# Weight-factor stores moved to GpSimd's queue, and a denser schedule of side work in the first attention

## The chip, the cores and the metric

One core of a Trainium2 chip runs the whole program. Its engines work side by side: TensorE (PE) multiplies matrices, VectorE (DVE) and ScalarE (ACT) do elementwise work, GpSimd (POOL) does a little of it and can issue DMAs, and SyncE (SP) does nothing but issue DMAs. The metric is the device time of one execution in microseconds (us). Before the change the median of three runs is 3205.84 us (3205.17 to 3208.25).

## The reference

The input x has 8 images of 512 channels and 32x32 positions (1024 tokens). Two layers of the same form follow each other; only the weights differ:

```python
xn  = group_norm(x, 8 groups) * gamma + beta
q, k, v = Wq @ xn + bq, Wk @ xn + bk, Wv @ xn + bv       # 512 x 512 each, 1024 tokens
attn = softmax(q_h^T k_h * 64**-0.5)                      # 8 heads of 64 channels
x   = x + Wp @ (attn @ v) + bp
```

All is float32. Eight images and two layers make 16 such jobs, and the kernel does them one after the other, two images at a time: layer 0 of images 0 and 1, then layer 1 of both, and so on.

## The kernel before

**Products by Strassen's scheme.** The four weight products of a job are done with seven block products in place of eight (Winograd's form), and for Q, K and the output projection O this is done twice, one level inside the other. That needs sums and differences of weight blocks ("factors") and of data blocks ("sums"). Four DVE subtractions or additions make the factors of a weight (`factor`, lines 154 to 160, parts 0 to 3). The first time a weight is used they are made from the raw blocks and stored to device memory (`store_factors`, L165 and L168); later `fetch` (L190) loads them into a ring of seven weight tiles. The factors of the second level are made in the ring the first time (`prepare`) and are stored by L204.

**Attention** (`class Attention`). A job's attention has 64 steps: 8 groups (head pair by half of the tokens) of 8 key blocks. Step i has four 64x512 score products (`sc`, L870), one exponential on ACT (`e`, L875), one addition on DVE that sums the exponentials over the key blocks (`acc`, L885 for the first of a group, L887 after it), and four products with the values two steps later (`po`, L901). The `e` tiles come from a pool of six, so that the exponential of step i+6 has to wait until the addition and the value products of step i have read theirs. At the end of a group `finish` reduces `acc` (L917) and adds the two halves of `po` (L924). After every second group the sums of 128 partitions are put together by three small DMAs (`r<-r`, L944), inverted on DVE (L948, L949), written to device memory (`rd`, L961), read back broadcast (`rb`, L963, two DMAs) and multiplied in (L978).

**Side work of an attention** (`chores`). The main loop gives each attention a table from step number to a piece of side work; `put(i, fn)` places a piece at step i, or at the next free step after it. For the first attention (n = 0) the table holds, in the order of placing: loading two raw weights (O of layer 0, V of layer 1) at step 2; their eight factor parts and two stores (`first_factors`); the statistics of the next job's group norm, which in this job alone are made on ACT (`reads`: four sums, the means, four sums of squares, and then one piece with a DVE scaling L258 and `gather`); and then `steps + sums`: `groups`, `factors` of the norm (L304 to L306), four ACT instructions that apply the norm (L311), and four DVE differences of blocks of the normalised input (`combine`, L385 to L391). Four inner differences (`inner_sums`, L423 to L429) come last.

**The chain of the group norm.** `gather` writes the statistics to device memory with two DMAs (`dm`, L275) and reads them back by groups (`gm`, L279). `groups` starts with a DVE instruction on `gm` (L286), ends with a power on GpSimd (L291), and its result goes out and back again (`dg`, L293; `mr`, L296) to the norm's factors (L304).

**Order.** The instructions of PE, ACT and DVE stand in the order in which the Python code issues them. Those of SP and POOL are ordered by the framework, from its own estimate of when each can run; every engine then works through its list strictly in order, and an instruction whose input is not there holds up all behind it on that engine.

Of the kernel before, what the change touches and what calls it, by code (L numbers as in the profile page):

```python
# [40 lines left out]
K, V, Q, O = range(4)  # L41
# [31 lines left out]
def fast_path(  # L73
# [10 lines left out]
    nc = tc.nc  # L84
# [23 lines left out]
    def later(delay, fn):  # L108
        todo.append((clock[0] + delay, fn))
# [36 lines left out]
    def load_blocks(w, layer, which):  # L146
        for i in range(2):
            for j in range(2):
                nc.sync.dma_start(w[:, 2 * j + i], raw_block(layer, which, i, j))

    def factor(w, part):

        if part == 0:
            nc.vector.tensor_add(w[:, S1], w[:, S3], w[:, A22])
        elif part == 1:
            nc.vector.tensor_sub(w[:, S2], w[:, S1], w[:, A11])  # L156
        elif part == 2:
            nc.vector.tensor_sub(w[:, S3], w[:, A11], w[:, S3])
        else:
            nc.vector.tensor_sub(w[:, S4], w[:, A12], w[:, S2])  # L160

    def store_factors(w, layer, which):
        keep = wdram.tile([P, NW, 2, CH], F32, name=f"keep_{which}_{layer}")
        if (which, layer) == (O, 1):
            nc.sync.dma_start(keep, w)  # L165
        else:
            for s in (slice(S1, NW), slice(S3, S3 + 1)):
                nc.sync.dma_start(keep[:, s], w[:, s])  # L168
        factors[which, layer] = keep

    plan, held, raw = deque(), {}, set()
# [1 line left out]
    def fetch():  # L173


        if not plan or len(held) == RING:
            return
        key = plan.popleft()
        n, which, o = key
        layer = jobs[n][1]  # L180
        w = ring.tile([P, NW, P], F32, tag="w", name=f"w_{which}_{n}_{o}")
        held[key] = w
        if (which, layer, o) in deep:
            nc.sync.dma_start(w, deep[which, layer, o])
        else:
            if o in BLOCK:
                src = raw_block(layer, which, *BLOCK[o])
            else:
                src = factors[which, layer][:, FACTOR[o]]
            nc.sync.dma_start(wide(w), src)  # L190
            if which != V:
                raw.add(key)
# [20 lines left out]
    def x_tile(b):  # L213
        xs[b] = xpool.tile([P, NC, S], F32, tag="x", name=f"x_{b}")
        return xs[b]

    def load_x(b):
        for cc in range(NC):
            nc.sync.dma_start(xs[b][:, cc, :], x[b, cc * P : (cc + 1) * P, :])

    class Norm:
# [20 lines left out]
        def sums(self, cc):  # L242

            nc.scalar.activation(
                xn[0][:, cc, :], xs[self.b][:, cc, :], AF.Identity, accum_out=self.mv[:, cc, 0:1]
            )
# [523 lines left out]
    def last_weights(n):  # L770
        w = acts.tile([P, NW, 2, CH], F32, tag="deep", name="w_last")
        nc.sync.dma_start(w, factors[O, jobs[n][1]])
        return w
# [10 lines left out]
    def last_sums(sh):  # L784


        def start():
            if sh == 0:
                tx[0] = acts.tile([P, 3, 2, HALF], F32, tag="t", name="t_last")
            nc.vector.tensor_sub(last_right(sh, 5), last_right(sh, 7), last_right(sh, 1))  # L790

        def second():
            nc.vector.tensor_sub(last_right(sh, 6), last_right(sh, 3), last_right(sh, 5))

        def third():
            nc.vector.tensor_sub(last_right(sh, 7), last_right(sh, 3), last_right(sh, 7))

        def fourth():
            nc.vector.tensor_sub(last_right(sh, 4), last_right(sh, 2), last_right(sh, 6))

        return start, second, third, fourth
# [241 lines left out]
    def deep_steps(n):  # L1043


        made = []

        def sums_(part, direct):
            if not made:
                made.append(True)  # L1050
                d = acts.tile([P, 4, 7, QT], F32, tag="deep", name=f"deep_{n}")
                deep_x[0], deep_t[0] = d[:, :, :4, :], d[:, :, 4:, :]
            inner_sums(part, direct)

        return [
            lambda part=part, direct=direct: sums_(part, direct)
            for direct in (True, False) for part in range(4)
        ]

    def extend_plan(n):  # L1060
        plan.extend((n, V, o) for o in ORDER)
        plan.extend((n - 1, O, o) for o in ORDER)
        plan.extend((n, which, o) for which in (K, Q) for o in OUTER)
# [29 lines left out]

        return load, [lambda oc=oc: add_up(oc) for oc in range(NC)]

    def first_factors(put, which_layers):

        box = []

        def start():  # L1100
            box.append(acts.tile([P, 2, NW, 2, CH], F32, tag="deep", name=f"raw_{len(factors)}"))
            for i, (which, layer) in enumerate(which_layers):
                load_blocks(box[0][:, i], layer, which)

        put(2, start)
        at = 9
        for i, (which, layer) in enumerate(which_layers):
            for part in range(4):
                at += 3
                put(at, lambda i=i, part=part: factor(box[0][:, i], part))  # L1110
            put(at + 1, lambda i=i, which=which, layer=layer: store_factors(
                box[0][:, i], layer, which
            ))

    deep_x, deep_t = [None], [None]
# [160 lines left out]
    for n in range(-1, len(jobs)):  # L1276
        last = n + 1 == len(jobs)
        outs = None
        if n >= 0:
            chores = {}  # L1280

            def put(i, fn):
                while i in chores:
                    i += 1
                chores[i] = fn

            if last:
                w = last_weights(n)
                for i, fn in enumerate(last_sums(0)):
                    put(44 + 3 * i, fn)  # L1290
            else:
                if n == 0:
                    first_factors(put, [(O, 0), (V, 1)])
                elif n == 1:
                    first_factors(put, [(K, 1), (Q, 1)])
                elif n == 2:
                    first_factors(put, [(O, 1)])
                for i, (_, fn) in enumerate(extra):
                    put(2 + i, fn)
                at = (10, 19, 22, 24, 26, 28, 36, 39, 42, 45)  # L1300
                if n == 0:
                    for i, fn in zip((3, 3, 4, 5, 6, 8, 10, 11, 12, 13, 15), reads):
                        put(i, fn)
                    at = (22, 30, 34, 35, 37, 38, 41, 44, 47, 50)
                for i, fn in zip(at, steps + sums(n + 1)):
                    put(i, fn)
                deep_first = deep_steps(n + 1)
                for at, fn in zip((52, 54, 57, 59), deep_first[4:]):
                    put(at, fn)
                put(61, lambda: (extend_plan(n + 1), [fetch() for _ in range(RING)]))  # L1310
            assert max(chores, default=0) < NT * len(att.groups)
            att.run(chores)
            banks(0, "one")
            banks(1, "one")
            if last:
                for i, fn in enumerate(last_sums(1)):
                    later(7.0 + 0.8 * i, fn)
                later(13.0, judge)
                for sh in range(2):
                    last_proj(n, w, sh)  # L1320
                break
            outs = OutputSums(n)
            out_sums(n, outs)
            first = v_phase(n + 1, ORDER)
            for thunk in first[:-1]:
                thunk()
            rest = first[-1:]
            extra = deque()
            if jobs[n][1] == 1 and jobs[n][0] + 2 < B:
                extra.append((11, lambda b=jobs[n][0] + 2: (x_tile(b), load_x(b))))  # L1330
            if n == 1:
                load, bias_steps = make_out_bias(1)
                extra.append((8, load))
                extra.extend((11, fn) for fn in bias_steps)
            if n + 2 < len(jobs):
                reads, steps = norm_steps(n + 2)
                extra.extend((15, fn) for fn in reads)
        both = deep_phases(n + 1, extra, outs, deep_first[:4] if outs else ())
        both[0]()
        rest[0]()  # L1340
        if n < 0:
            later(22.0, lambda: load_x(1))
        for thunk in both[1:]:
            thunk()
        banks(0, "two")
        att = Attention(n + 1)
        att.scores(0)
        att.scores(1)
        banks(1, "two")
        att.scores(2, "po")  # L1350
# [249 lines left out]
```

## Time and profile before

| what | value |
|---|---|
| median of three runs | 3205.84 us (3205.17 to 3208.25) |
| the profiled execution | 3206.06 us, span 3204.3 us |
| busy, of the span | PE 99%, DVE 87%, ACT 60%, POOL 3% |
| granted TensorE clock | 1.00 throughout |
| one attention, first score product to last value product | 109.6 us the first, 109.5 us all others |
| from there to the next attention's first score product | 96.0, 93.1, 90.6 us after the first three, 88.3 us after nearly all others |

The span is the time from the first to the last instruction of the program; the time of the execution holds 1.8 us more. Busy time is what instructions of an engine took together; an engine's "wait" is time in which it stood idle, put down to whatever ended it.

### The profile page before, as it was taken

The page shows a single profiled execution, that of the slowest core. Times are in us where ns is not written, and L with a number is a line of the kernel's source. Part 1 is how long each engine was busy: PE and PEld are TensorE (multiplying, and loading weights), DVE is VectorE, ACT ScalarE, POOL GpSimd, SP SyncE. Part 2 cuts the span into 40 slices and gives each one's busy share as a digit, 9 for nine tenths or more (in the row PEclk, how much of TensorE's full clock was granted, in tenths as well). Part 3 has the DMA queues.
Part 4 walks back from the last instruction along what each step waited for, and adds up shares of the span by engine and source line. Part 5 has one row for each costly group of instructions (what it writes and reads, how often), then busy time and mean ns, then how long its engine had stood idle before and what let it go on. Part 6 is the DMA issues. An engine that isn't in the chain of part 4 may idle for free.

```text
span 3204.3 us, 57789 instructions
## 1 busy us (share of the span) xinstructions
PE 3185.3 (99%) x22917; PEld 1862.8 (58%) x22917; DVE 2772.8 (87%) x3989; ACT 1914.4 (60%) x3063; POOL 100.7 (3%) x95
## 2 busy tenths in 40 slices
PE   9999999999999999999999999999999999999999
PEld 7366384563836638366483754837547375573744
DVE  8897999979889798897988879888898888978878
ACT  4746646466565665656656565565656656566564
POOL 0000000000000000000000000000000000000000
PEclk9999999999999999999999999999999999999999
DMA  8234172350613305034170421504316051150611
GB/s 291 74 107 127 48 213 70 92 169 22 210 28 88 91 26 159 22 100 132 33 211 16 114 72 33 152 16 135 103 44 194 16 137 48 49 136 16 174 37 42
DMA packets 156998, 308.32 MB, mean 96 GB/s; under 512 B 34104, under 2 KB 60592, under 8 KB 156464
## 3 DMA queue, kind: packets, MB, share of 16 engines
q1 hardware_dynamic: 139856, 272.05, 26.8%
q0 software_dynamic: 16864, 32.51, 6.2%
q8 instruction: 181, 2.97, 0.4%
q14 instruction: 97, 0.79, 0.1%
HBM read 225.13 MB, written 45.68 MB: 85 GB/s over the span
## 4 chain that ended last, share of the span: by engine, by line
PE 95%; DVE 3%; DMA 1%; issue 0%; POOL 0%; ACT 0%; DVEq 0%; ACTq 0%; POOLq 0%
PE sc L870 28%; PE po L901 27%; PE zd L636 10%; PE vd L636 10%; PE z L494 6%; PE yd L636 5%; PE ud L636 4%; PE v L494 2%; PE y L494 2%; PE u L494 1%; PE z_last L814 0%; DMA x<-p 0%; DVE w L156 0%; DMA w<-deep 0%; DVE p L655 0%; DVE v L520 0%
## 5 line engine op out<-in xcount | busy, mean ns | idle before, releaser
L875 ACT ACTIVATE e<-sc 128x1024 f32<-128x1024 f32 x1024 | 1045.3, 1025 | 563.4 <-PE sc L870 457.4
L870 PE MATMUL sc<-q,k 64*64 64x512 f32 x8192 | 1058.0, 589 | 0.0
L901 PE MATMUL po<-e,v 64*64 64x512 f32 x8192 | 1057.1, 589 | 0.0
L887 DVE TENSOR_TENSOR acc<-acc,e 128x1024 f32<-128x1024 f32 x768 | 936.0, 1219 | 58.8 <-ACT e L875 12.1
L901 PEld LDWEIGHTS po<-e,v 64*64 64x64 f32 x8192 | 312.9, 133 | 566.0 <-issue 554.4
L870 PEld LDWEIGHTS sc<-q,k 64*64 64x64 f32 x8192 | 311.2, 133 | 562.7 <-issue 545.0
L885 DVE TENSOR_TENSOR acc<-e,e 128x1024 f32<-128x1024 f32 x128 | 156.3, 1221 | 112.3 <-ACT e L875 112.2
L636 PE MATMUL zd<-deep,w 128*128 128x256 f32 x860 | 241.1, 380 | 3.8 <-DVE p L653 1.7
L636 PE MATMUL vd<-deep,w 128*128 128x256 f32 x804 | 224.3, 380 | 2.1 <-DVE p L655 1.3
L636 PEld LDWEIGHTS zd<-deep,w 128*128 128x128 f32 x860 | 162.8, 190 | 28.2 <-DVE p L653 3.0
L636 PEld LDWEIGHTS vd<-deep,w 128*128 128x128 f32 x804 | 152.3, 190 | 24.6 <-DVE p L655 2.5
L917 DVE TRANSPOSE_TENSOR_REDUCE r<-acc 128x32 f32<-128x1024 f32 x128 | 158.5, 1238 | 0.6
L682 POOL DMA_DIRECT2D x<-p x62 | 74.6, 1211 | 1972.7 <-ACT p L646 1525.2
L636 PE MATMUL vd<-os,w 128*128 128x256 f32 x420 | 118.1, 380 | 1.6 <-DVE p L655 1.5
L668 DVE TENSOR_TENSOR p<-p,p 128x1024 f32<-128x1024 f32 x94 | 114.2, 1214 | 0.0
L494 PE MATMUL z<-w,t 128*128 128x256 f32 x480 | 110.9, 379 | 0.0
L494 PE MATMUL z<-w,xn 128*128 128x256 f32 x480 | 110.1, 382 | 0.0
L518 ACT COPY v<-z 128x512 f32<-128x512 f32 x32 | 18.8, 586 | 148.7 <-PE z L494 148.7
L494 PEld LDWEIGHTS z<-w,xn 128*128 128x128 f32 x480 | 90.0, 190 | 23.8 <-issue 12.2
L442 ACT COPY ud<-zd 128x256 f32<-128x256 f32 x156 | 55.7, 357 | 76.6 <-PE zd L636 75.1
L653 DVE TENSOR_TENSOR p<-vd,s 128x256 f32<-128x256 f32 x63 | 26.7, 424 | 85.6 <-PE vd L636 85.6
L657 ACT COPY s<-vd 128x256 f32<-128x256 f32 x156 | 58.1, 373 | 69.2 <-PE vd L636 69.2
(242 smaller groups left out, 4194.9 us busy)
## 6 DMA issues: line engine op xcount, KB each, us to landing
w<-deep SPq DMA_DIRECT2D x287, 448.0 KB, 3.8
x<-p POOLq DMA_DIRECT2D x62, 512.0 KB, 6.9
rb<-rd SPq DMA_DIRECT2D x96, 256.0 KB, 4.0
w<-keep SPq DMA_DIRECT2D x84, 256.0 KB, 2.7
deep<-w SPq DMA_DIRECT2D x42, 448.0 KB, 3.8
w<-wqkv_dram SPq DMA_DIRECT2D x57, 256.0 KB, 2.8
x<-x_dram SPq DMA_DIRECT2D x28, 512.0 KB, 6.4
out_dram<-x SPq DMA_DIRECT2D x28, 512.0 KB, 6.2
```

Source lines behind the costliest of these rows:

```text
L442: nc.scalar.copy(u, z)
L494: nc.tensor.matmul(ps[:, ti * CH : (ti + 1) * CH], right(src, tx[0], o)[:, cc, t0 : t0 + P], w[:, cc, :], start=(start and ti == 0 and cc ...
L636: nc.tensor.matmul(ps, lhs[:, FACTOR[i], :], moving[i], start=start, stop=True, skip_group_check=True,)
L657: return chain(product, lambda ps: nc.scalar.copy(s5, ps), put, z, y, u, w)
L668: outer.append(lambda: nc.vector.tensor_add(to_, a, b))
L682: nc.gpsimd.dma_start(to_, p(part), accum_op=ALU.add)
L870: nc.tensor.matmul(sc[h * HD : (h + 1) * HD, j, :], k[r, hp, k0 : k0 + HD], q[r, hp, sh * HALF : (sh + 1) * HALF], start=True, stop=True,)
L875: nc.scalar.activation(e, sc, AF.Exp, scale=SCALE)
L885: nc.vector.tensor_add(acc[g], self.es[i - 1], e)
L887: nc.vector.tensor_add(acc[g], acc[g], e)
L901: nc.tensor.matmul(po[g][j * HD : (j + 1) * HD, h, :], v[r, kc, d0 : d0 + HD], e[r, j, :], start=(kc == 0), stop=(kc == NT - 1),)
L917: nc.vector.tensor_reduce(self.r[:, 0, m, :], self.acc.pop(g).rearrange("p j (b e) -> p (j b) e", e=RP), AX.X, ALU.add, apply_transpose=True,)
```

## The change

Three things change. `store_factors` takes the queue on which it issues, and the two or one stores per weight that the first three attentions make go to GpSimd's queue (five weights: two in the first, two in the second, one in the third); the three stores ahead of the first attention stay on SP. In the first attention the factor parts start at step 8 and come every second step (before: step 12, every third). And in the first attention the block differences and the inner differences of the next job are placed closer together and earlier.

```diff
-    def store_factors(w, layer, which):
+    def store_factors(w, layer, which, queue=nc.sync):
         keep = wdram.tile([P, NW, 2, CH], F32, name=f"keep_{which}_{layer}")
         if (which, layer) == (O, 1):
-            nc.sync.dma_start(keep, w)
+            queue.dma_start(keep, w)
         else:
             for s in (slice(S1, NW), slice(S3, S3 + 1)):
-                nc.sync.dma_start(keep[:, s], w[:, s])
+                queue.dma_start(keep[:, s], w[:, s])
         factors[which, layer] = keep
...
-    def first_factors(put, which_layers):
+    def first_factors(put, which_layers, at=9, apart=3):
...
         put(2, start)
-        at = 9
         for i, (which, layer) in enumerate(which_layers):
             for part in range(4):
-                at += 3
+                at += apart
                 put(at, lambda i=i, part=part: factor(box[0][:, i], part))
             put(at + 1, lambda i=i, which=which, layer=layer: store_factors(
-                box[0][:, i], layer, which
+                box[0][:, i], layer, which, nc.gpsimd
             ))
...
                 if n == 0:
-                    first_factors(put, [(O, 0), (V, 1)])
+                    first_factors(put, [(O, 0), (V, 1)], 6, 2)
...
                 if n == 0:
                     for i, fn in zip((3, 3, 4, 5, 6, 8, 10, 11, 12, 13, 15), reads):
                         put(i, fn)
-                    at = (22, 30, 34, 35, 37, 38, 41, 44, 47, 50)
+                    at = (22, 30, 34, 35, 36, 37, 39, 41, 43, 45)
                 for i, fn in zip(at, steps + sums(n + 1)):
                     put(i, fn)
                 deep_first = deep_steps(n + 1)
-                for at, fn in zip((52, 54, 57, 59), deep_first[4:]):
+                for at, fn in zip((47, 49, 51, 53) if n == 0 else (52, 54, 57, 59), deep_first[4:]):
                     put(at, fn)
```

## The prediction

> **What bounds the kernel now.** First the page's head:
>
> ```profile
> span 3204.3 us, 57789 instructions
> PE 3185.3 (99%) x22917; PEld 1862.8 (58%) x22917; DVE 2772.8 (87%) x3989; ACT 1914.4 (60%) x3063; POOL 100.7 (3%) x95
> ```
>
> TensorE is the bound, so only a TensorE gap can be won or lost. Where are they? The busy time by stage (stretch; then busy us and count for PE, PEld, DVE, ACT, POOL; then clock, DMA share and GB/s):
>
> ```profile
> 81.50:191.10 109.60, 109.60 (x1023) 38.96 (x1024) 99.06 (x121) 80.77 (x92) 2.07 (x1) 1.00 0.19 59
> 191.10:287.10 96.00, 90.33 (x418) 76.38 (x410) 80.01 (x153) 46.57 (x116) 6.18 (x5) 1.00 0.57 163
> ...
> 396.60:489.70 93.10, 90.40 (x414) 76.34 (x406) 86.43 (x189) 46.51 (x116) 4.80 (x4) 1.00 0.65 195
> ...
> 599.20:689.80 90.60, 89.27 (x415) 76.61 (x407) 77.18 (x151) 46.60 (x116) 6.00 (x5) 1.00 0.71 218
> ...
> 799.30:887.60 88.30, 88.30 (x414) 77.00 (x406) 72.14 (x124) 46.60 (x116) 4.80 (x4) 1.00 0.66 197
> ```
>
> The attentions have no gap. The stretches between them (weight products) take 96.0, 93.1 and 90.6 us after the first three and 88.3 us once all is in step: 7.7 + 4.8 + 2.3 = 14.8 us in all that this kernel could win, 0.46%. What ends the gaps of the first such stretch (192 to 250 us, waits of PE):
>
> ```profile
> PE zd L636 <- DVE p L653: 1.7, 2, 1.1
> PE v L494 <- DVE q L924: 1.7, 1, 1.7
> PE zd L636 <- ACT yd L438: 1.6, 1, 1.6
> ```
>
> DVE is behind: the first value product of the next job waits 1.7 us for the last `q` (L924) of the first attention. After that the trace shows no idle time of DVE until 235.2 us, so up to there TensorE runs at DVE's pace: the pieces by which this stretch lags a settled one are 1.9 us at its start, 2.5 us up to 230, and 3.1 us at 243 to 249, where DVE's own gaps name accumulating DMAs (`x<-p`). The first 4.4 us fall if DVE ends the attention sooner, and grow if it ends later. So: when is DVE idle in the first attention (81.5 to 198 us, waits of DVE)?
>
> ```profile
> DVE acc L887 <- ACT e L875: 3.1, 6, 0.8
> DVE lt L948 <- DMA r<-r: 2.5, 1, 2.5
> DVE acc L885 <- ACT e L875: 2.4, 2, 1.6
> ```
>
> 8.0 us, all before 121 us; from there on it always has work. The DMA wait comes from SP's list (start, duration):
>
> ```profile
> 110.43 1.36 SPq L275 DMA_DIRECT2D dm<-mv  x2
> 116.76 0.38 SPq L279 DMA_DIRECT2D gm<-dm  x1
> 117.24 2.28 SPq L944 DMA_DIRECT2D r<-r  x3
> 119.63 0.53 SPq L168 DMA_DIRECT2D keep<-raw  x1
> 122.38 0.34 SPq L961 DMA_DIRECT2D rd<-rt  x1
> 124.94 1.30 SPq L963 DMA_DIRECT2D rb<-rd  x2
> ```
>
> The norm's statistics (`dm`, then `gm`) stand ahead of `r<-r`, and `gm` waits 4.9 us for `dm` to land. The `keep` stores hold up nothing: SP waits for their factors, but what is behind them would wait longer for DVE anyway. On DVE, 16 us pass between the scaling that starts the chain (L258) and its reader L286:
>
> ```profile
> 110.20 0.16 DVE L258 TENSOR_SCALAR mv<-mv 128x8 f32<-128x8 f32 x1
> ...
> 126.71 0.21 DVE L286 BATCH_NORM_STATS2 gs<-gm 8x6 f32<-8x64 f32 x1
> ```
>
> **What the Trainium skill says.** "DMA: Bandwidth & Descriptors", section "Issuing engines are not separate DMA queues": DMAs of SP and GpSimd run on the same 16 DMA engines and interleave, so another issuer only saves issuing time. The trace prices that at 0.3 to 0.5 us of SP per `keep` store, on a queue that is not the bound. Same page, "Anatomy of one DMA": most of a DMA's fixed 2 us is the wait until the last byte is confirmed, longest where the target is device memory. The trace agrees: `r<-r` (chip memory) lands 1.8 to 2.2 us after issue, `dm` (device memory) after 3.7 to 6.7. "SBUF — State Buffer", "SBUF: two separate sides": GpSimd cannot write DMA descriptors while DVE runs an instruction in a two-port mode. The trace of before shows GpSimd's DMAs at 1.2 us of issue each beside a busy DVE, so I take 1.2.
>
> **The change, part by part.**
>
> *Stores on GpSimd.* Nine DMAs (four, four, one) leave SP and cost GpSimd 9 x 1.2 = 11 us; it is 97% idle. In the first attention its list becomes four stores, then the power L291: the last store waits for a factor (L160) that stands well ahead of L290 on DVE, so the power is not held up. In the second and third attention the power stands before the stores, the accumulating DMAs long after, and SP's stores delayed nothing there (TensorE has no gap in those attentions). I take 0. If that cover failed, a late power would delay L304 to L306; it has about 4 us of room in my sum below.
>
> *Factors sooner.* Same eight DVE instructions of 0.60 us (start to start). They now begin at step 8, where DVE still waits for exponentials: waits of 1.6, 0.3, 0.2 and 0.8 us (97 to 109 us) can be filled. With two per group between dependent additions, which otherwise stand 0.2 us apart, I take 1.6 + 0.3 = 1.9 us of idle time gained.
>
> *What that pushes.* The statistics are placed after the factors, and `put` moves a piece on when its step is taken. Worked through: the last square moves from step 14 to 19, L258 with `gather` from 16 to 21, but `groups` only from 23 to 24. The seven steps between the chain's start and its reader become three. In the changed kernel's order DVE has between L258 and L286 only two additions and one factor. SP's list there is now: `r<-r` x3, `rd`, `dm`, `rb` x2, `dm`, `gm`, `dg`. So `r<-r` no longer waits (2.5 us of DVE gained), but the second `dm` stands behind 512 KB of `rb`, beside the 768 KB store on GpSimd's queue.
>
> The new wait, from durations of before: L948 follows the addition of step 20 (ends 118.3) and a factor: 118.9. L948 to L968 take 1.7 us, so the addition of step 21 begins at 120.6, L258 ends at 121.9, and with addition, factor, addition (1.2 + 0.6 + 1.2) DVE stands at L286 at 124.8. The first `dm` is issued at 121.9, `rb` twice (0.65 each) from 122.6, the second `dm` at 123.9 to 124.5. Before, `gm` could be issued 5.5 us after the second `dm` (111.19 to 116.73); with 1.5 us for queueing that is 131.0. Landing of `gm`: at most 2.5 us in the second attention (issue 304.50, L286 at 307.01 without a wait); I take 2.1. L286 at 133.2: **a wait of 8.4 us.** Bounds: no queueing and a quick confirmation as elsewhere (`dm` in 3.7) 5.3; the full 4 us for which `rb` and the store kept the DMA engines busy in the trace of before (126.5 to 130.8), 10.9.
>
> *Differences sooner* (steps 39 to 45 and 47 to 53). The same eight DVE instructions in another order; DVE is never idle there, so its end doesn't move: 0. If DVE did have idle time near the end, this part would gain; in the trace it has none after 121 us.
>
> **Sum.** DVE's end of the first attention: +8.4 - 2.5 - 1.9 = +4.0; I add 0.2 for waits behind the gaps that TensorE itself now gets: +4.2. Where it is late next: six `e` tiles let ACT run ahead, but the exponential of step 30 is due at 134.0 (81.5 + 30 x 1.7125 + 1.16) and the addition that frees its tile ends at 135.2. Then the norm's factors: 10.5 us of DVE work after L290 puts L306 at 144.5 to 145, and the ACT instruction that applies the norm stands ahead of the exponential of step 35, due at 142.6. So TensorE loses some 3 to 4 us inside the attention, and less at its end. Up to 230 it follows DVE; the DMAs behind the 3.1 us follow DVE's products too. So all +4.2 reaches the end. Against the profiled 3206.06 us that makes 3210.3; this execution is 0.2 above the median, so **3210.0 us**.
>
> 0.2% (6.4 us) is about what a measurement of this kernel can tell from no change.
>
> **Rivals.**
>
> *The chain is later: slower by over 0.2%.* From a wait of about 10.6 us the sum passes 6.4. The upper bound does it: second `dm` and `gm` each behind full DMA engines, 10.9 - 4.4 + 0.2 = +6.7, 3212.5 us; every further us adds one. For it: the order of SP's list and 1.3 MB within 4 us. Against: the small DMAs share the engines packet by packet. Chance 0.25.
>
> *The change does what it looks like it does.* If `gm` landed soon after 124.8, only the gains remain: -4.4 + 0.2, 3201.6 us. Against: 2.9 us from L258 to L286 for a chain that took 6.3 before up to the issue of `gm` alone (110.43 to 116.76). To pass -6.4 the `x<-p` gaps (3.1 us) would have to go as well. Chance 0.10 for any gain of 1 us or more, 0.03 for over 0.2%.
>
> *A wait that just cancels.* At a wait of 4.2 us nothing is left, 3206 us; it shades into the lower bound (5.3: +1.1). It is part of "no change".
>
> *GpSimd's stores starve* because DVE locks its port: then the power comes late. Room 4 us, and beyond it us for us. Chance 0.03, in the slower share.
>
> **How the numbers follow.** Likeliest: a wait between 5.3 and 10.6 us, +1 to +6, chance 0.62, within 0.2%. Slower by over 0.2%: 0.25 + 0.03 = 0.28. Faster: 0.03. Within: 0.69. The range leaves out under one in ten on each side: low 3204.5 (the lower bound less the spread of the runs), high 3213.5 (the upper bound plus 1).
>
> **What would show it.** Right: L286 waits 5 to 11 us for `gm` in the first attention; no wait at L948; that attention takes 112 to 114 us in place of 109.6, with gaps near steps 30 to 40; the stretch after it about 96 to 97; the second and third attention and all later stages as before; no `keep` on SP. Wrong: no wait at L286 and a first stretch of about 92; or changed stretches after the second or third attention, which would mean that the stores mattered.

## The result, and the profile after

The changed kernel takes 3214.23 us, the median of 10 runs (3212.83 to 3215.85). The kernel before, run beside it, takes 3205.06 us (10 runs, 3204.44 to 3208.25). The ratio is 1.0028, with a 95% interval of 1.0019 to 1.0036: slower by 0.28%, 9.2 us, where no measurable change was forecast. The median lies 0.7 us above the upper end of the forecast range. The profiled execution of the changed kernel took 3213.18 us, with a span of 3211.4 us, against 3206.06 and 3204.3 before: this pair of profiles shows 7.1 us of the loss, because the profiled run after is 1.0 below its median and the one before 1.0 above.

The head of the page after. TensorE is still busy 99% of the time, so the share hides the loss, but the microseconds show it: outside its busy time are 24.5 us of the span, where it was 19.0 before, and the busy time itself grew by 1.6:

```profile
span 3211.4 us, 57792 instructions
PE 3186.9 (99%) x22917; PEld 1862.3 (58%) x22917; DVE 2773.2 (86%) x3989; ACT 1914.3 (60%) x3063; POOL 104.5 (3%) x104
```

Busy time by stage after (stretch in us from the span's start and its length; then busy us and count for PE, PEld, DVE, ACT, POOL; then clock, DMA share and GB/s): first attention, the stretches behind the first, second and third, and a settled stretch.

```profile
80.70:198.30 117.60, 112.39 (x1025) 38.93 (x1024) 99.53 (x122) 80.68 (x92) 3.89 (x5) 0.99 0.19 55
198.30:293.10 94.80, 90.25 (x414) 76.34 (x406) 79.44 (x152) 46.58 (x116) 6.03 (x5) 1.00 0.57 164
402.60:496.10 93.50, 90.64 (x417) 76.28 (x409) 86.60 (x189) 46.52 (x116) 4.77 (x4) 1.00 0.66 195
605.60:697.10 91.50, 89.39 (x414) 76.59 (x406) 77.68 (x151) 46.60 (x116) 5.86 (x5) 1.00 0.71 216
806.60:894.90 88.30, 88.30 (x414) 77.00 (x406) 72.17 (x124) 46.60 (x116) 4.73 (x4) 1.00 0.66 197
```

The first attention grew from 109.6 to 117.6 us (+8.0), and the stretch behind it shrank from 96.0 to 94.8 (-1.1 from the unrounded starts). The second and third attention took 109.5 as before. The stretches behind them are longer by 0.3 and 0.9 us, which is within what the third one does from run to run (90.2 to 91.7 in 13 of the 14 profiles of this study); the same kernel run again (e9, below) is slower than before in neither of them by more than 0.1 us. The settled stretch is unchanged. So the loss is the first attention's. What DVE waited for in it, after:

```profile
DVE gs L286 <- DMA gm<-dm: 11.6, 1, 11.6
DVE acc L885 <- ACT e L875: 2.0, 2, 1.0
DVE acc L887 <- ACT e L875: 1.8, 3, 0.7
```

The wait for `r<-r` (2.5 us before) is gone, and a wait of 11.6 us for `gm` stands in its place. DVE's list shows the two ends of it (start, duration, line and operation, and in brackets the idle time and what ended it):

```profile
120.86 0.15 DVE L258 TENSOR_SCALAR mv<-mv 128x8 f32<-128x8 f32 x1
121.04 1.23 DVE L887 TENSOR_TENSOR acc<-acc,e 128x1024 f32<-128x1024 f32 x1
122.18 0.68 DVE L160 TENSOR_TENSOR raw<-raw 128x512 f32<-128x512 f32 x1
122.78 1.22 DVE L887 TENSOR_TENSOR acc<-acc,e 128x1024 f32<-128x1024 f32 x1
135.57 0.22 DVE L286 BATCH_NORM_STATS2 gs<-gm 8x6 f32<-8x64 f32 x1 [11.57 <-DMA gm<-dm]
```

Between the start of the norm's chain (L258) and its reader (L286) stand three instructions. SP's list in the same stretch says what the chain went through (start, duration):

```profile
119.58 0.35 SPq L961 DMA_DIRECT2D rd<-rt  x1
121.08 0.68 SPq L275 DMA_DIRECT2D dm<-mv  x1
121.85 2.52 SPq L963 DMA_DIRECT2D rb<-rd  x2
124.42 1.34 SPq L275 DMA_DIRECT2D dm<-mv  x1
132.55 0.36 SPq L279 DMA_DIRECT2D gm<-dm  x1
```

The second `dm` was issued behind `rb`, and `gm` could be issued only 8.1 us after it (132.55 - 124.42), where before the change it took 5.5 (111.19 to 116.73). What TensorE and ACT waited for in the first attention, after, in two views:

```profile
PE sc L870 <- ACT e L875: 4.9, 2, 4.6
```

```profile
ACT e L875 <- DVE acc L885: 6.7, 1, 6.7
ACT e L875 <- DVE acc L887: 2.1, 1, 2.1
ACT xn L311 <- DVE off L306: 1.3, 1, 1.3
```

DVE's idle time reaches TensorE through the `e` tiles: an exponential waits for the addition that frees its tile, and the score product waits for the exponential. That is 4.9 of the 8.0 us, 4.6 of it in one wait. TensorE's list shows a second part:

```profile
133.12 1.04 PE L901 MATMUL po<-e,v 64*64 64x512 f32 x8
138.75 1.82 PE L870 MATMUL sc<-q,k 64*64 64x512 f32 x8 [4.59 <-ACT e L875]
140.33 1.95 PE L901 MATMUL po<-e,v 64*64 64x512 f32 x8
```

Eight value products took 1.04 us ahead of the gap and 1.95 behind it. The granted clock explains it (busy time by stretch, columns as above; the clock is the third number from the end):

```profile
139.00:142.40 3.40, 3.40 (x20) 1.07 (x16) 3.29 (x4) 1.35 (x2) 0.00 (x0) 0.50 0.04 6
142.40:146.00 3.60, 3.60 (x36) 1.23 (x32) 3.29 (x4) 2.75 (x4) 0.00 (x0) 1.00 0.00 0
```

For 3.4 us TensorE ran at half clock, which costs 1.7 us of its time. The remaining 1.4 us of the 8.0 (8.0 - 4.9 - 1.7) come from ACT somewhat later. After its wait for the norm's factors (the 1.3 us above) it has four steps with two pieces of work each, one application of the norm and one exponential:

```profile
147.39 1.24 ACT L311 ACTIVATE xn<-x,off,mul 128x1024 f32<-128x1024 f32 x1 [1.33 <-DVE off L306]
148.54 1.00 ACT L875 ACTIVATE e<-sc 128x1024 f32<-128x1024 f32 x1
149.44 1.23 ACT L311 ACTIVATE xn<-x,off,mul 128x1024 f32<-128x1024 f32 x1
```

So its exponentials come 2.0 us apart where a step of TensorE takes 1.7, and TensorE's score products start 0.3 to 0.5 us later at each of these four steps. By these starts it is 1.5 us in all, part of it in pauses too short for the list of waits.

Behind the attention, TensorE's waits (192 to 262 us) look like those of before: the first value product again waits for the last `q`, 1.1 us (1.7 before), and DVE's products `p` stand for most of the rest.

```profile
PE zd L636 <- DVE p L653: 2.3, 2, 1.6
PE v L494 <- DVE q L924: 1.1, 1, 1.1
PE vd L636 <- DVE p L655: 0.6, 1, 0.6
PE zd L636 <- ACT yd L438: 0.4, 1, 0.4
```

### The profile page after: what moved, and what is told of

Its sections match the earlier page's. It is cut to its first block, busy times and chain, and to the rows that moved or that the text cites. A ratio compares the mean times of both kernels' runs of the same rounds, so it can differ in the third digit from the quotient of the medians.

```text
span 3211.4 us, 57792 instructions
## 1 busy us (share of the span) xinstructions
PE 3186.9 (99%) x22917; PEld 1862.3 (58%) x22917; DVE 2773.2 (86%) x3989; ACT 1914.3 (60%) x3063; POOL 104.5 (3%) x104
## 4 chain that ended last, share of the span: by engine, by line
PE 92%; DVE 6%; DMA 1%; issue 1%; ACT 0%; SPq 0%; POOL 0%; DVEq 0%; ACTq 0%; POOLq 0%
PE sc L870 26%; PE po L901 26%; PE zd L636 10%; PE vd L636 10%; PE z L494 6%; PE yd L636 5%; PE ud L636 4%; PE v L494 2%; PE y L494 2%; PE u L494 1%; DVE acc L887 1%; PE z_last L814 0%; DMA x<-p 0%; DMA w<-deep 0%; DVE w L156 0%
```

## The experiments

All kernels below compute everything that the reference asks. Four were run on one chip, four on a second and four on a third, each set beside the kernel before (3205.09, 3204.94 and 3205.15 us there). The table gives the time, the ratio to the kernel before, and from the profile: DVE's idle time in the first attention (gaps over 0.3 us), the end of DVE's last `q` (L924) counted from the attention's start, and the distance from the attention's first score product to that of the next attention. The last three columns are of one profiled execution each; that of before was 1.0 us above its median, and those of e1 and e4, with the same steps around `gather` and `groups`, have about 1 us less idle time.

| kernel | median us | ratio, 95% interval | DVE idle | last `q` ends at | to next attention |
|---|---|---|---|---|---|
| before | 3205.06 | | 7.55 | 117.2 | 205.6 |
| after | 3214.23 | 1.0028, 1.0019 to 1.0036 | 15.42 | 124.6 | 212.4 |
| e9: after again | 3214.16 | 1.0029, 1.0018 to 1.0040 | 16.65 | 125.8 | 213.2 |
| e1: stores alone | 3205.78 | 1.0002, 0.9994 to 1.0011 | 6.59 | 116.2 | 204.4 |
| e2: schedule alone | 3212.08 | 1.0022, 1.0014 to 1.0030 | 14.91 | 124.1 | 212.5 |
| e11: e2 again | 3213.43 | 1.0026, 1.0016 to 1.0037 | 15.97 | 125.2 | 213.1 |
| e4: differences alone | 3204.39 | 0.9998, 0.9990 to 1.0007 | 6.72 | 116.4 | 204.0 |
| e5: chain starts first | 3204.61 | 0.9999, 0.9991 to 1.0008 | 5.88 | 115.2 | 203.4 |
| e8: reader 2 steps later | 3209.60 | 1.0014, 1.0007 to 1.0020 | 12.03 | 121.6 | 209.2 |
| e3: reader 7 steps later | 3211.21 | 1.0020, 1.0012 to 1.0028 | 12.33 | 121.7 | 209.3 |
| e6: chain on GpSimd's queue | 3209.78 | 1.0015, 1.0008 to 1.0021 | 12.84 | 122.0 | 210.4 |
| e7: e5 and e6 together | 3203.18 | 0.9994, 0.9986 to 1.0003 | 5.28 | 114.8 | 203.1 |
| e12: e7 again | 3203.39 | 0.9993, 0.9985 to 1.0002 | 5.28 | 114.8 | 202.5 |
| e10: e7, factors in gaps | 3203.05 | 0.9992, 0.9984 to 1.0001 | 4.77 | 114.8 | 202.9 |

Two things hold in all fourteen profiles. The last `q` ends 109.2 to 110.0 us after the attention's start plus DVE's idle time in it (after: 124.6 - 15.4 = 109.2; e10: 114.8 - 4.8 = 110.0). And the next attention starts 87.4 to 88.4 us after that `q` (after: 212.4 - 124.6 = 87.8). The first is close to bookkeeping, since DVE does the same work in every kernel. The second is the finding: whatever else happened, TensorE's gaps and half clock included, DVE's idle time in the first attention came out at the other end about one to one.

### e1 and e2: which part of the change costs?

e1 keeps the stores on GpSimd's queue and puts the old steps back:

```diff
-                    first_factors(put, [(O, 0), (V, 1)], 6, 2)
+                    first_factors(put, [(O, 0), (V, 1)])
...
-                    at = (22, 30, 34, 35, 36, 37, 39, 41, 43, 45)
+                    at = (22, 30, 34, 35, 37, 38, 41, 44, 47, 50)
...
-                for at, fn in zip((47, 49, 51, 53) if n == 0 else (52, 54, 57, 59), deep_first[4:]):
+                for at, fn in zip((52, 54, 57, 59), deep_first[4:]):
```

> Only the stores go to GpSimd's queue; the first attention's table is that of the kernel before. Theory (the loss is DVE's wait for the norm's statistics, which comes from the table alone): 3205 to 3207 us, as before, first attention 109.6 us, DVE waits 2.5 us for r<-r and nothing for gm. Rival (GpSimd's stores starve, or the 768 KB store in flight beside small DMAs costs by itself): 3208 us or more.

e2 keeps the new steps and puts the stores back on SP:

```diff
-                box[0][:, i], layer, which, nc.gpsimd
+                box[0][:, i], layer, which
```

> Only the table changes; the stores stay on SP, where the order now puts the 768 KB store of V behind the second dm and ahead of gm. Theory A (the wait at L286 comes from three steps between L258 and L286, whoever stores): the wait is there, 9 to 12 us, and the time is 3212 to 3216 us. Theory B (the store on GpSimd's queue, ahead of rb and the second dm on the DMA engines, made a good part of it): the wait is 7 to 9 us and the time 3208 to 3211 us.

Measured: e1 3205.78 us, no difference from before; e2 3212.08, slower by 0.22%, as theory A had it. The steps carry the loss, and the queue of the stores costs nothing that can be seen by itself. DVE's wait for `gm` in e2 is 11.1 us although its last 768 KB store stands behind the second `dm` on SP. e2 came out 2.1 us under the changed kernel, so both were run again beside each other (e9 and e11, below).

### e4: the differences sooner, alone

The kernel before with only this edit:

```diff
-                    at = (22, 30, 34, 35, 37, 38, 41, 44, 47, 50)
+                    at = (22, 30, 34, 35, 36, 37, 39, 41, 43, 45)
...
-                for at, fn in zip((52, 54, 57, 59), deep_first[4:]):
+                for at, fn in zip((47, 49, 51, 53) if n == 0 else (52, 54, 57, 59), deep_first[4:]):
```

> The kernel before with only the block and inner differences placed sooner. Theory: DVE is never idle from 121 us on, so 3205 to 3207 us, no change, q L924 still 1.7 us late for the first value product. Rival (sooner differences free the end of the attention): 3203 us or less, and that wait gone.

Measured: 3204.39 us, ratio 0.9998: no difference. With e1 this leaves the factors' steps, and what they push, as the one part that costs.

### e5: the same dense factors, but the norm's chain starts first

A rival to the wait was that eight factors at every second step are simply too dense beside the additions. e5 places the statistics ahead of the factors, so that L258 and `gather` come at step 15, and leaves L286 at step 24. The factors then take the next free steps and come out denser still, seven of the eight between steps 14 and 22:

```diff
+                    for i, fn in zip((3, 3, 4, 5, 6, 8, 10, 11, 12, 13, 15), reads):
+                        put(i, fn)
                     first_factors(put, [(O, 0), (V, 1)], 6, 2)
...
-                    for i, fn in zip((3, 3, 4, 5, 6, 8, 10, 11, 12, 13, 15), reads):
-                        put(i, fn)
```

> The changed kernel, with the norm's statistics placed ahead of the factors: L258 and gather at step 15 in place of 21, L286 where it is in the changed kernel (step 24, the same neighbours on DVE), stores on GpSimd. Theory (the loss is the short way from L258 to L286): no wait for gm, the wait for r<-r of the kernel before is back (1 to 3 us), no dip of the clock in the first attention, which takes 109.6 us; 3203 to 3206 us. Rival (the factors' or the differences' new places cost by themselves): 3208 us or more.

Measured: 3204.61 us, ratio 0.9999: the whole loss is gone. DVE's list in e5 shows the chain's reader without a wait, and its start 16.7 us ahead of it:

```profile
110.92 0.16 DVE L258 TENSOR_SCALAR mv<-mv 128x8 f32<-128x8 f32 x1
...
127.59 0.21 DVE L286 BATCH_NORM_STATS2 gs<-gm 8x6 f32<-8x64 f32 x1
```

So dense factors are harmless, and the late start of the chain is the cause. This run and the changed kernel are the pair that shows it; e2 shows that the queue of the stores has no part in it. Starting the chain at step 15 does two things at once: it gives `gather` nine steps up to `groups` in place of three, and it takes `dm` away from `rb`. The next three runs look at the two apart.

### e3 and e8: the reader later instead

If three steps are too short, moving `groups` back should help as well. e3 moves it by seven steps, e8 by two, each with what follows it:

```diff
-                    at = (22, 30, 34, 35, 36, 37, 39, 41, 43, 45)
+                    at = (31, 35, 36, 37, 38, 39, 41, 43, 45, 47)
```

> The changed kernel, with groups at step 31 in place of 24 and what follows it moved on by one or two steps (factors of the norm 35, the four applications 36 to 39, the block differences 41 to 47, the inner ones 49 to 55). Theory (one wait is the whole loss): no wait at L286 or under 1 us, first attention 109.5 us, no dip of the granted clock in it, DVE ends it 4 us sooner than before, 3201 to 3203 us. Rival (the denser side work itself is the loss): 3208 us or more.

```diff
-                    at = (22, 30, 34, 35, 36, 37, 39, 41, 43, 45)
+                    at = (26, 32, 34, 35, 36, 37, 39, 41, 43, 45)
```

> The changed kernel with groups at step 26 in place of 24 and the norm's factors at 32 in place of 30, the rest unmoved. Theory: DVE waits in two places (L978 for rb, L286 for gm), 6 to 8 us in all; with additions done between them the exponentials go on, TensorE's gap falls under 3 us and the clock does not dip; 3207 to 3210 us. If the dip and not the wait makes the loss it falls further, to 3205.

e3 missed: 3211.21 us, where 3201 to 3203 had been expected. Ten steps between `gather` and `groups` are not enough by themselves. DVE's waits in e3:

```profile
DVE q L978 <- DMA rb<-rd: 4.8, 1, 4.8
DVE acc L885 <- ACT e L875: 4.1, 3, 2.1
```

The wait for `gm` is gone, but DVE now reaches L978, the next reader of something that was in flight at that time, and waits there: `rb` is late too. And by moving the norm's factors (L304 to L306) to one step ahead of ACT's use of them (L311), e3 made a second stall, which TensorE feels:

```profile
ACT xn L311 <- DVE off L306: 5.0, 1, 5.0
```

ACT stood 5.0 us at L311 with exponentials queued behind it, TensorE's longest wait was 4.0 us, and its clock fell. DVE then waited for late exponentials (the 4.1 us above). (e3's profiled execution, 3213.64 us, is its slowest; 3 us of it lie in the stretch behind the third attention, where none of the other profiles has them.)

e8 came out at 3209.60 us, inside what was expected. Its DVE waits show the same `rb`, now ahead of the reader of `gm`:

```profile
DVE q L978 <- DMA rb<-rd: 6.1, 1, 6.1
...
DVE gs L286 <- DMA gm<-dm: 1.0, 1, 1.0
```

Together 7.1 us. So the stall goes with `dm` and `rb` being in flight together; moving one reader shows the other. One part of e8's expectation failed: TensorE still had a gap of 3.2 us, and its clock fell for 6.8 us. So e8 does not tell the half clock from the wait; e6 does.

### e6: the chain on GpSimd's queue

Is it the order in SP's list? e6 takes the new steps with the stores on SP, and issues `dm`, `gm`, `dg` and `mr` of this one job on GpSimd's queue, so that no `dm` stands behind `rb` (lines of the helper move by two):

```diff
+            q = nc.gpsimd if self.n == 1 else nc.sync
...
-                nc.sync.dma_start(
+                q.dma_start(
...
-            nc.sync.dma_start(self.gm, dm.rearrange("h c p k -> (h c) p k"))
+            q.dma_start(self.gm, dm.rearrange("h c p k -> (h c) p k"))
...
```

> The changed kernel's table, stores on SP, and the norm's DMAs of this one job (dm, gm, dg, mr) on GpSimd's queue, so that rb and the second dm no longer stand behind each other in one list. Theory A (a dm in SP's queue holds back what is issued behind it, and this made half of the chain): rb lands within 4 to 5 us of its issue in place of 8, gm lands 9 us after L258, the wait at L286 is 6 to 8 us, TensorE's gap is under 3 us and the clock does not dip; 3206 to 3209 us. Theory B (the chain has its length anyway): wait 10 us or more, 3211 us or more.

Measured: 3209.78 us, between what the two theories gave. GpSimd's list, then DVE's:

```profile
121.27 1.49 POOL L276 DMA_DIRECT2D dm<-mv  x2 [103.51 <-DVE mv L258]
127.82 0.56 POOL L280 DMA_DIRECT2D gm<-dm  x1 [5.06 <-DMA dm<-mv]
```

```profile
132.63 0.21 DVE L288 BATCH_NORM_STATS2 gs<-gm 8x6 f32<-8x64 f32 x1 [8.98 <-DMA gm<-dm]
```

Both `dm` are out by 122.76 and `gm` goes out at 127.82, 4.4 us sooner than after, counted from the attention's start (80.4 against 80.7); yet L288 gets it only 4.8 us later, where it took 3.0 after. The wait is 9.0 us instead of 11.1 to 12.8. Order in one queue explains a part, 2 to 4 us. The rest is there with separate queues too: in e6 the two `rb` still landed 6.0 and 9.5 us after issue, where in e7, with `dm` eleven us away, they took 3.8 and 5.0. `dm` took 5.5 and 5.2 us (3.2 to 4.0 on that queue in e7, e12 and e10), and `gm`, now in flight beside the second `rb` and the 768 KB store, 4.8 (2.2 to 2.6 there). What slows them (the tiny pieces of `dm`, the device memory, or the shared DMA engines) was not separated and stays open. Device memory alone is not enough: `rd`, 8 KB, is written there too and landed 1.4 us after issue in this run.

e6 also settles a rival, that TensorE's half clock is the loss: in its first attention the granted clock stayed at 1.00 (the longest gap was 2.0 us), and it still loses 4.8 us.

### e9 and e11: the changed kernel and the schedule alone, side by side

e9 is the changed kernel, e11 is e2.

> The changed kernel once more, beside the next one on the same chip. If the stores' queue costs nothing: within 1 us of the kernel with the table alone, 3212 to 3213 us. If GpSimd's 768 KB store, which stands ahead of rb and the second dm on the DMA engines, costs what the earlier medians differ by: 2 us more than that kernel, 3214 us.

> The kernel with the new table alone and all stores on SP, once more: 3211 to 3213 us, DVE idle some 15 us in the first attention, 11 of them at L286.

Measured: 3214.16 and 3213.43 us. The 2.1 us between the first pair did not come back; 0.7 us is left, and the intervals overlap; e11 lies 0.4 us above what was expected. What did come back is the spread of the wait itself: 11.1 and 12.1 us in e2 and e11, 11.6 and 12.8 in the changed kernel. The longest of these, in e9's list of DVE waits:

```profile
DVE gs L286 <- DMA gm<-dm: 12.8, 1, 12.8
```

e9's profiled span is 3213.6 us, 9.3 more than before, which is the whole loss of the medians. The four runs also answer whether the 768 KB store holds up the second `dm`: in after and e9 it is issued ahead of that `dm`, in e2 and e11 behind it, and from the issue of that `dm` to that of `gm` pass 8.1 and 10.0 us with the one order and 9.5 and 10.2 with the other. Its place makes no difference that can be seen.

### e7, e12 and e10: is there a version that beats both?

e7 takes the order of e5 and the queue of e6, with the stores on SP. e12 is e7 once more. e10 also runs the four factor parts of O beside the statistics at steps 6 to 9, where DVE waits for exponentials.

> Both of these together: statistics ahead of the factors, their DMAs on GpSimd's queue, stores on SP. Theory: neither L286 nor L948 waits for a DMA, DVE ends the first attention 3 to 4 us sooner than before, 3200 to 3203 us. Rival (the stores on SP now delay r<-r in their turn, or the end is bound by something else): 3204 us or more.

> Statistics first and their DMAs on GpSimd's queue, stores on SP, once more: 3202 to 3204 us, 1 to 3 us under the kernel before.

> Statistics first and their DMAs on GpSimd's queue, stores on SP, and O's four factor parts in the very first gaps of DVE (steps 6 to 9, beside the statistics' work on ACT). Theory (the end of the first attention is 109.5 us plus DVE's idle time in it): idle time 3 to 4 us in place of 7.6 before and 5.3 without this step, 3200 to 3202 us. Rival (the end is no longer DVE's): 3203 us or more.

Measured: 3203.18, 3203.39 and 3203.05 us, 1.8 to 2.1 us under the kernel before; each interval just reaches 1, so none is shown faster by itself. e7 lies 0.2 us above what was expected, e12 inside it. e12's stages, first attention and the stretch behind it:

```profile
81.20:190.90 109.70, 109.70 (x1025) 38.80 (x1024) 101.57 (x123) 80.67 (x92) 5.17 (x7) 1.00 0.19 59
190.90:283.67 92.77, 89.55 (x415) 76.51 (x407) 77.62 (x151) 46.49 (x116) 6.08 (x5) 1.00 0.58 168
```

and DVE's waits in that attention (e7; the lines are those of `e` and its additions, moved by two):

```profile
DVE acc L889 <- ACT e L877: 3.4, 6, 0.8
DVE acc L887 <- ACT e L877: 2.1, 3, 1.6
```

No DMA wait is left, and the stretch has come from 96.0 to 92.8 us. e10 missed: it was to bring DVE's idle time to 3 to 4 us and the time to 3200 to 3202, and its 3203.05 us is where its rival began. Idle time fell to 4.8 us only, because filling the early gaps moved idle time to a later addition, which then waited 1.3 us for its exponential (0.3 in e7), and the last `q` ended no sooner (114.8 in both). At that addition ACT sets the pace; this earlier side work did not make DVE end sooner.

## Why the prediction was wrong, step by step

**What bounds the kernel: right.** The table bears out that DVE's end in the first attention sets the start of the next attention, 87.4 to 88.4 us later, and that all of a delay of DVE reaches the end: +7.4 us at the last `q`, +6.9 at the next attention.

**Stores on GpSimd, 0: right.** e1, e9 and e11. The price taken, 1.2 us of issue each, was too high: those of the first attention took 0.54 to 0.77 us of GpSimd. The lock of which the Trainium skill speaks ("SBUF — State Buffer", "SBUF: two separate sides") did not show: e1 has these stores beside a DVE that is over 90% busy and loses nothing. Whether any of DVE's instructions there runs in the two-port mode that the page means, no run here tells. The second and third attention, and the later stages, are as before, as predicted.

**Factors sooner, 1.9 us: right in kind, too large.** DVE's waits for ACT fell from 5.0 to 3.9 us (gaps over 0.3), by 1.2. The `r<-r` wait of 2.5 us went, as predicted; but it is itself not fixed, since e1 and e4, with `dm`, `gm` and `r<-r` in the same order on SP as before, show 1.6 and 1.7.

**Differences sooner, 0: right** (e4).

**The new wait at L286, 8.4 us: right place and cause, wrong size. This is the step that failed.** Counted from the attention's start (which was 0.8 us earlier than before), DVE reached L286 at 43.3 us, exactly as worked out. The 3.2 us between 8.4 and 11.6 are three terms. The second `dm` was issued 1.3 us later than taken (43.7 against 42.4), as the two `rb` took 2.52 us of SP and not 1.3. From that issue to that of `gm` passed 8.1 us where the sum had 7.1. And `gm` took 3.0 us from issue to its reader, not 2.2. In the other three profiles with this schedule the middle term is the largest: 9.5, 10.0 and 10.2 us (e2, e9, e11). The sum put 1.5 us on top of the undisturbed 5.5 for queueing; measured is 2.6 to 4.7. The upper bound put 4.0 there and took everything else as undisturbed, so it was no bound: 10.9 was passed in all four profiles.

**Inside the attention, 3 to 4 us lost by TensorE: too small,** 8.0. The larger wait accounts for most of it; the norm's late factors, which the prediction named, make some 1.5, and the half clock, which it did not have, adds 1.7. But this is not added to the total: what TensorE lost inside beyond DVE's own delay came back as a shorter stretch (94.8 where 96 to 97 had been said), because DVE's end decides.

**The choice among the cases.** The mechanism of the likeliest case and of the rival "the chain is later" is one, and only the wait's size decides between them, at about 10.6 us. The rival gave 3212.5 us and holds, 1.7 us short of the median. Taking 1.5 us, on the ground that "the small DMAs share the engines", was a choice without a row of the trace behind it: no stage of the profile before had `dm` in flight with `rb`, and the one row that showed a loaded `dm` (3.7 to 6.7 us to land) already said that its time can nearly double. The prediction also read the long landing of `dm` as that of device memory; `rd`, which is written there too, landed in 2.5 us before and 1.4 after, about as soon as `r<-r`, so device memory alone does not explain it.

## What to carry to other kernels

When side work is pushed along a table of steps, look at the distance between the start of every DMA chain and its first reader, not at the pieces that were moved on purpose; an in-order engine that stands at the reader loses the whole difference. Where a chain's small DMAs come to lie beside a large transfer that they were far from before, take no undisturbed time for either, and look for the second reader: moving the first one (e3, e8) only shows the other. The cure that worked was to start the chain earlier (e5).

## What was not expected of the hardware

**Half clock behind a gap.** In the first attention the granted clock fell to 0.50 for 3.4 us (after, e2, e3) or 6.8 us (e8, e9, e11), each time in or behind an idle time of TensorE of 3.2 to 5.8 us. e8's stretch:

```profile
147.00:153.80 6.80, 5.91 (x28) 1.79 (x32) 6.52 (x11) 6.49 (x7) 0.00 (x0) 0.50 0.02 4
```

The Trainium skill ("TensorE: Matmul & The Clock Gate", "Part 1: The HAM clock gate") gives half rate after an idle window of about 3.4 us, with windows that run freely. The traces agree with the length of the steps, 3.4 us or twice that. They differ at the edge: a gap of 3.2 us (e8) and one of 2.4 us (e3, behind the third attention, at 680 us) were followed by half clock too, and gaps of up to 2.0 us (e6; 1.7 before the change) were not. In the first 15 us of four runs (after, e1, e4, e5) the clock was also at half for 3.4 or 6.8 us, with no single wait of TensorE over 1.5 us ahead of it. Where DVE was the later engine anyway, the lower clock cost nothing at the end: the next attention starts 87.4 us behind the last `q` in e9, with 6.8 us of half clock, and 88.4 in e6, with none.

**Two kinds of DMA that slow each other.** Landing times are those at which the trace shows the last update of a DMA's semaphore. `dm`, which writes a few bytes per piece into device memory, landed 3.2 to 5.9 us after issue away from `rb` (before, e1, e4, e5, e7), and 6.2 and 8.1 us after it in the changed kernel, with `rb` in flight; in e9, the same kernel, 5.9 and 10.0. `rb`, 256 KB each, took 3.5 to 5.0 us away from `dm` (once 5.9, in e1, beside the 768 KB store), up to 10.4 us with `dm` in flight (e9, e11), and 9.5 on another queue than `dm` (e6). `rb` is not the only large transfer that this can meet: in e5 a 256 KB store on GpSimd's queue, issued beside `dm`, took 6.4 us, where such a store took 2.3 and 2.5 us in the changed kernel; in e7 one issued with `dm` took 2.0, so being in flight together is not always enough.
